# Chunks of at most four gathered rows from a tile pool and a split last superblock, in place of a ring of 50 slots with chunks of up to eight

## The chip, the cores and the metric

The kernel runs on 1 core of one Trainium2 chip. The metric is the device time in microseconds; the time of a kernel is the median of its runs, and lower is better.

## The reference, cut to what matters

A two-layer heterogeneous graph transformer over N = 6250 nodes and E = 100000 edges (sorted by destination), with 16 node types, 32 edge types, width D = 128 and H = 8 heads of 16; around it stands `layernorm(x + gnn(x))`.

```python
def gt_layer(x, ntype, etype, src, dst, Wk, Wq, Wv, Wa, Watt, Wmsg, pri, skip, g, b):
    k = typed_linear(x, ntype, Wk)          # (n, 8, 16); q and v alike
...
    kT = jnp.einsum('nhd,htdo->nhto', k, Watt)      # for each node and edge type
    vT = jnp.einsum('nhd,htdo->nhto', v, Wmsg)
    kw = kT[src, :, etype]
    m = vT[src, :, etype]
    a = jnp.einsum('ehd,ehd->eh', kw, q[dst]) * pri[:, etype].T / SQRT_D
    att = edge_softmax(a, dst, n)
    hag = jax.ops.segment_sum((m * att[:, :, None]).reshape(-1, H * HS), dst, num_segments=n)
    h = jax.nn.silu(typed_linear(hag, ntype, Wa))
    alpha = jax.nn.sigmoid(skip[ntype])[:, None]
    h = h * alpha + x * (1.0 - alpha)
    return normalised(h) * g + b
h = x
for l in range(2): h = gt_layer(h, ...)
return layernorm(x + h @ ff_w + ff_b)
```

## The kernel before, in words

**Prep.** Nodes are ranked by class of types (4 classes of 4 types) and by degree into 50 blocks of 128 nodes, one node to a partition. Block b has `KB[b]` slots, the most incoming edges of any of its nodes: 25, 22, 20, 19, 18, 17, 16, 16, 15, 14 in each class's ten blocks, and 41, 13, 12, 12, 12, 11, 11, 10, 9, 8 in ten blocks of mixed types; 867 in sum. A table in DRAM (`tabs[l]`) holds one row of 256 floats, k and v after `Watt` and `Wmsg`, for every node and edge type. Layer 0's table is written during prep (L1000), in tiles `st` of 2 MB, two to a block.

**Edges of a layer** (`edges(l)`). Blocks come in superblocks of up to four (`sbs`): for each class 4, 3 and 3 blocks, and a superblock of mixed blocks after each of the first three classes, 15 in all. The last two are blocks 34 to 36 and 37 to 39 (K of the latter 16, 15, 14). For each slot of a block one indirect DMA, issued by POOL, gathers 128 rows of the table, one to a partition (L1270): 867 gathers a layer. A block's slots are cut into chunks. For each chunk DVE multiplies k by q (L1282) and sums over each head to `a` (L1286). When all chunks of a block are there, the generator `finished` does the rest: mask, maximum, subtraction, exponential (ACT, L1166), denominators, then the values times weights (L1185), their sum over chunks in `acc` (L1196) and over the chunk's rows (L1201). In layer 0, q, weights and `acc` lie in SBUF; in layer 1 in PSUM (a `tb` tile, `pair`). `finished` of one block is called step by step (`step`) while the next block's chunks are emitted (`before`).

**The ring.** Gathered rows lie in `kvr`, a ring of `SLOTS` = 50 rows. A block's chunks are even, of up to `MOST` = 8 rows, split where the ring ends; 135 chunks a layer. If a slot is still to be read, `finished` of the block before is driven on until its value is added (`used`, `live`).

**Nodes.** After a superblock's last block, the generator `nodes` is put on the list `work`: normalise, transpose, the typed product with `Wa` (L276), silu by tanh, skip, layer norm (`stats`, L1347 and L1350; `rstd_of`), and in layer 0 the next layer's k, v and q (three products, in this order), q written to DRAM (`qrd`). Then `table(pieces_of(...))` puts the pieces of layer 1's table on the list `pieces`: PE products (L297), copies to `st` (ACT, L304; some on DVE, L302), and a scatter by POOL (L1479), `late` by three half steps. `tick` advances `work` and `pieces` at a pace set by the slots of the coming superblocks; `queries` of the next superblock are on `work` too. What is left when the gathers are out is drained at the end of the layer. Layer 1's first gather waits for all scatters of its table. In layer 1, `nodes` ends in `ff_w`, the residual and the last layer norm, giving `o` (L1465); `results` holds its blocks, `leave` counts them down from 7 + 2i and `put_out` writes them by an indirect DMA on POOL (L1512); those of the last superblock are written at once.

**Order.** POOL's instructions run in the order of the program (`manual_schedule` for POOL); an instruction that waits there holds all later gathers, scatters and outs. The other engines' instructions are put in order by the tile framework's scheduler.

Of the kernel before, what the change touches and what calls it, by code (L numbers as in the profile page):

```python
# [9 lines left out]
F32 = mybir.dt.float32  # L10
# [3 lines left out]
ALU = mybir.AluOpType  # L14
# [17 lines left out]
CH = 4  # L32

MOST = 8

SLOTS = 50

# [80 lines left out]
def kernel(  # L118
# [136 lines left out]
    def superblocks(n):  # L255
        k = -(-n // SB)
        for c in range(k):
            yield n * c // k, n * (c + 1) // k - n * c // k
# [773 lines left out]
    def arm(fast):  # L1032
# [4 lines left out]
        STB = 3 if fast else 2  # L1037
        room = [0]
        ep = ctx2.enter_context(tc.tile_pool(name="ep", bufs=2))
        npl = ctx2.enter_context(tc.tile_pool(name="npl", bufs=1))  # L1040
        if fast:
            kvr = npl.tile([P, SLOTS, 2 * D], F32, name="kv")
        eps = npl.tile([P, 1], F32, name="eps")
# [7 lines left out]
        if fast:  # L1051

            mixed = [(NC * CB + i0, k, range(TY)) for i0, k in superblocks(1 + RB)]
            for c in range(NC):
                for i0, k in reversed(list(superblocks(CB))):
                    sbs.append((c * CB + CB - i0 - k, k, range(c * TC, (c + 1) * TC)))
                sbs += mixed[c * len(mixed) // (NC - 1):(c + 1) * len(mixed) // (NC - 1)]
        else:
            sbs = [(i0, k, range(TY)) for i0, k in superblocks(NB)]
# [40 lines left out]
        def edges(l):  # L1100
# [27 lines left out]

            def leave(n):

                for r in results:
                    r[0] -= n
                if results and results[0][0] <= 0:
                    put_out(*results.pop(0)[1])

            def slots(s):
                return sum(KB[b] for b in range(sbs[s][0], sbs[s][0] + sbs[s][1]))

            live = []

# [8 lines left out]

            def finished(s, i, chunks, kvt, used, a, pair, sums, den):  # L1150

# [22 lines left out]
                else:  # L1174
                    acc = pair[:, 0].rearrange("p (k c) -> p k c", k=CH)
                late = []
                for j in range(len(chunks) + 1):
                    more = []
                    if j < len(chunks):
                        j0, j1 = chunks[j]  # L1180
                        v = kvt[j][:, :, D:]
                        parts = [(0, j1 - j0)] if j else [
                            (k0, min(k0 + CH, j1 - j0)) for k0 in range(0, j1 - j0, CH)]
                        for k0, k1 in parts:
                            nc.vector.tensor_tensor(  # L1185
                                (v[:, k0:k1] if j or k0 else acc[:, :k1])
                                .rearrange("p k (h d) -> p k h d", h=H),
                                v[:, k0:k1].rearrange("p k (h d) -> p k h d", h=H),
                                w[:, j0 + k0:j0 + k1, :].unsqueeze(3)
                                .to_broadcast([P, k1 - k0, H, HS]), op=ALU.mult)  # L1190
                        more = [v[:, k0:min(k0 + CH, j1 - j0)]
                                for k0 in range(0 if j else CH, j1 - j0, CH)]
                        yield
                    for v in late:
                        n = v.shape[1]
                        nc.vector.tensor_tensor(acc[:, :n], v, acc[:, :n], op=ALU.add)  # L1196
                    late = more
                    for r in used[:j]:
                        r[2] = True
                    yield  # L1200
# [24 lines left out]
            for s, (i0, k, types) in enumerate(sbs):  # L1225
# [6 lines left out]
                for i in range(k):  # L1232
                    b = i0 + i
                    K = KB[b]
                    a = ep.tile([P, max(KB), H], F32, name="a")
                    if SLOTS - room[0] < CH:
                        room[0] = 0
                    most = min(K, SLOTS - room[0])
                    chunks = []
                    for k0, k1 in ((0, most), (most, K)):  # L1240
                        n = -(-(k1 - k0) // MOST)
                        chunks += [(k0 + (k1 - k0) * j // n, k0 + (k1 - k0) * (j + 1) // n)
                                   for j in range(n)]
                    kvt, used = [], []
                    then = []
# [11 lines left out]
                    for j0, j1 in chunks:  # L1257
                        c = j1 - j0
                        for r in [r for r in live if r[0] < room[0] + c and r[1] > room[0]]:
                            while not r[2]:  # L1260
                                next(before)
                            live.remove(r)
                        live.append([room[0], room[0] + c, False])
                        used.append(live[-1])
                        kv = kvr[:, room[0]:room[0] + c]
                        room[0] = (room[0] + c) % SLOTS
                        kvt.append(kv)
                        for j in range(j0, j1):
# [4 lines left out]
                            if l == 1:  # L1273
# [6 lines left out]
                                puts.clear()  # L1280
                        kk = kv[:, :, :D]
                        nc.vector.tensor_tensor(  # L1282
                            kk, kk, q.unsqueeze(1).to_broadcast([P, c, D]), op=ALU.mult)
                        for r in range(c):
                            if r == c // 3:
                                nc.vector.tensor_reduce(  # L1286
                                    a[:, j0:j1, :], kk.rearrange("p k (h d) -> p k h d", h=H),
                                    axis=AX.X, op=ALU.add)
                            step()
                            tick(1.0)  # L1290
                        leave(c / CH)
                    for _ in before:
                        pass
                    if not then:
                        step(end=True)
                    before = finished(s, i, chunks, kvt, used, a, pair, sums, den)
                    q, pair = then[0] if then else (None, None)
# [55 lines left out]
        def nodes(l, i0, k, types, sums, den, ntb, table):  # L1353
# [45 lines left out]
            if not last:  # L1399
# [22 lines left out]
                elif fast:  # L1422
# [4 lines left out]
                    outs = []  # L1427
                    for j in range(3):
                        ps = nps.tile([P, SB * P], F32, name="nb")
                        outs.append(ps)  # L1430
                        for t, xm in xms:
                            nc.tensor.matmul(ps[:, :n], wkqv[:, j, t, :], xm[:, :n],
                                             start=(t == types[0]), stop=(t == types[-1]))
                        yield
                        if j < 2:
                            to = npl.tile([P, SB * P], F32, name=f"kvT{j}", bufs=2)
                            nc.scalar.copy(to[:, :n], ps[:, :n])
                            outs[j] = to
# [9 lines left out]
                nc.sync.dma_start(rows(qrd[1], i0, k), q[:, :k])  # L1448
                table(pieces_of(i0, k, outs[0], outs[1], (2,) if final else ()))
                return  # L1450
# [229 lines left out]
```

## Time and profile before

| | us |
|---|---|
| median of 3 runs (lowest, highest) | 3686.52 (3684.35, 3697.19) |
| the profiled execution, its own time | 3697.19 |
| the profiled execution, its span | 3695.1 |
| POOL busy, 2213 instructions | 2152.3 |
| DVE busy, 4025 instructions | 1951.6 |
| PE busy | 1808.3 |
| ACT busy | 1018.3 |
| first gather of layer 1 | 2279.99 |

The profiled execution is the highest of the three runs. Busy time leaves out the issue of DMAs and waits. A line of the table of groups has the source line, the engine, the operation, the tiles (out<-in), the count, the busy time, the mean ns of one, and the idle time of the engine ahead of them with what ended it; a line of the waits has engine, tile and line, what ended the wait, us in total, times, longest; a line of a timeline has start, duration, the instruction, and the engine's idle time before it. The granted TensorE clock is 0.64 over the span.

### The profile page before, as it was taken

How to read it: one execution, taken by the hardware profiler on the slowest of the kernel's cores; microseconds unless marked ns; L12 is line 12 of the kernel's file. 1: busy time of each engine (PE TensorE's matmuls, PEld its weight loads, DVE VectorE, ACT ScalarE, POOL GpSimd, SP SyncE). 2: the span in 40 equal slices, each digit the busy share in tenths (PEclk: the TensorE clock that was granted, in tenths of full speed). 3: DMA queues.
4: the chain of work that ended last, by engine and by line, in shares of the span. 5: the costliest groups of instructions: out<-in, count | busy, mean ns of one | idle time of the engine just before them, and what ended most of it. 6: DMA issues, size and time to landing. Idle time of an engine off the chain costs nothing. (4 is left out here: it accounts for less than half of the span.)

```text
span 3695.1 us, 22082 instructions
## 1 busy us (share of the span) xinstructions
PE 1808.3 (49%) x5612; PEld 825.1 (22%) x5612; DVE 1951.6 (53%) x4025; ACT 1018.3 (28%) x1677; POOL 2152.3 (58%) x2213
## 2 busy tenths in 40 slices
PE   3898998115556587668776774012120212113113
PEld 1344545002223233223222221001010101111011
DVE  8665331356356565567456442445554556464545
ACT  2675655002331344123331542001110111111111
POOL 2224654674676666667676543755767557666653
PEclk9788675557667686777768776555555555555555
DMA  6797999634655577456765686332333223333321
GB/s 181 308 387 312 400 403 404 169 99 145 224 188 192 179 266 266 156 171 241 271 220 172 221 307 255 107 87 82 102 93 105 83 86 104 94 90 97 90 82 44
DMA packets 194484, 691.11 MB, mean 187 GB/s; under 512 B 55469, under 2 KB 106032, under 8 KB 169298
## 3 DMA queue, kind: packets, MB, share of 16 engines
q0 software_dynamic: 119120, 651.15, 49.8%
q1 hardware_dynamic: 58838, 31.29, 3.2%
q10 hardware_dynamic: 16384, 7.11, 0.9%
q8 instruction: 48, 0.79, 0.1%
q14 instruction: 94, 0.77, 0.1%
HBM read 264.91 MB, written 429.48 MB: 188 GB/s over the span
## 5 line engine op out<-in xcount | busy, mean ns | idle before, releaser
L1270 POOL DMA_INDIRECT kv<-tab,ell x1734 | 1726.4, 996 | 656.8 <-issue 486.3
L304 ACT COPY st<-tb 128x512 f32<-128x512 f32 (+1 forms) x1064 | 726.4, 758 | 506.7 <-PE tb L297 252.0
L282 PE MATMUL nb<-ident,hag 128*128 128x128 f32 x100 | 25.8, 396 | 765.3 <-DVE hag L1318 207.7
L297 PE MATMUL tb<-bdv,kvT 32*128 32x512 f32 x800 | 283.8, 852 | 96.2 <-ACT st L304 56.9
L297 PE MATMUL tb<-bdv,vT 32*128 32x512 f32 x784 | 296.6, 884 | 28.5 <-ACT st L304 16.9
L1282 DVE TENSOR_TENSOR kv<-kv,q 128x896 f32<-128x896 f32 (+4 forms) x135 | 136.6, 1012 | 315.5 <-DMA kv<-tab,ell 276.2
L276 PE MATMUL nb<-xm,wa 128*128 128x384 f32 (+1 forms) x384 | 236.8, 775 | 131.8 <-DVE xm L267 85.4
L297 PE MATMUL tb<-bdk,kvT 32*128 32x512 f32 x800 | 267.6, 838 | 65.9 <-ACT st L304 46.5
L1479 POOL DMA_INDIRECT tab<-st,row x100 | 105.3, 1053 | 316.4 <-ACT st L304 260.6
L1286 DVE TENSOR_REDUCE a<-kv 128x48 f32<-128x768 f32 (+4 forms) x269 | 270.6, 1007 | 31.3 <-remote 24.2
L267 DVE SCALAR_TENSOR_TENSOR xm<-ntb,nb 128x384 f32<-128x384 bf16 (+1 forms) x336 | 184.7, 595 | 176.5 <-remote 78.0
L297 PE MATMUL tb<-bdk,kT 32*128 32x512 f32 x784 | 257.6, 865 | 0.3 <-ACT st L304 0.3
L1282 DVE TENSOR_TENSOR kv<-kv,tb 128x768 f32<-128x768 f32 (+4 forms) x134 | 136.0, 1015 | 219.4 <-DMA kv<-tab,ell 176.1
L1000 POOL DMA_INDIRECT tab<-st,rows x98 | 103.3, 1054 | 242.4 <-ACT st L304 210.1
L282 PE MATMUL nb<-ident,hs 128*128 128x128 f32 x100 | 37.9, 459 | 328.8 <-DVE hs L1391 158.7
L302 DVE COPY st<-tb 128x512 f32<-128x512 f32 (+1 forms) x120 | 89.1, 745 | 201.6 <-PE tb L297 133.1
L282 PEld LDWEIGHTS nb<-ident,hag 128*128 128x128 f32 x100 | 15.6, 196 | 784.1 <-issue 571.1
L276 PE MATMUL nb<-xm,wq 128*128 128x384 f32 (+1 forms) x192 | 104.6, 707 | 120.3 <-DVE xm L267 108.4
L1512 POOL DMA_INDIRECT out_dram<-o,node x50 | 50.9, 1018 | 192.6 <-DVE o L1465 180.8
L276 PEld LDWEIGHTS nb<-xm,wa 128*128 128x128 f32 x384 | 99.8, 280 | 265.1 <-issue 123.5
L1196 DVE TENSOR_TENSOR tb<-kv,tb 128x512 f32<-128x512 f32 (+3 forms) x211 | 121.9, 578 | 56.2 <-remote 39.2
L1413 PE MATMUL nb<-xm,wkqv 128*128 128x384 f32 (+1 forms) x288 | 122.6, 582 | 39.2 <-DVE xm L267 24.7
(314 smaller groups left out, 2829.8 us busy)
## 6 DMA issues: line engine op xcount, KB each, us to landing
kv<-tab,ell POOLq DMA_INDIRECT x1734
hr<-xrd SPq DMA_DIRECT2D x30, 192.0 KB
hr<-xrd SPq DMA_DIRECT2D x15, 256.0 KB
xrd<-xr POOLq DMA_DIRECT2D x11, 256.0 KB
ntb<-typed SPq DMA_DIRECT2D x20, 96.0 KB
hrd<-hs SPq DMA_DIRECT2D x10, 192.0 KB
qrd<-q SPq DMA_DIRECT2D x10, 192.0 KB
q<-qrd SPq DMA_DIRECT2D x10, 192.0 KB
```

The lines of the kernel that those rows point to most:

```text
L267: nc.vector.scalar_tensor_tensor(xm[:, :n], ntb[:, :n], float(t), hT[:, :n], op0=ALU.is_equal, op1=ALU.mult)
L276: nc.tensor.matmul(ps[:, :n], w[:, t, :], xm[:, :n], start=(t == types[0]), stop=(t == types[-1]))
L297: nc.tensor.matmul(pt[:, b], yT[s, i * P:(i + 1) * P], bd[s, tt, :], start=True, stop=True)
L302: nc.vector.tensor_copy(to, pt)
L304: nc.scalar.copy(to, pt)
L1000: put = nc.gpsimd.indirect_dma_start(out=tabs[0].rearrange("(n t) c -> n (t c)", t=16), out_offset=bass.IndirectOffsetOnAxis(ap=rows1[:, t ...
L1196: nc.vector.tensor_tensor(acc[:, :n], v, acc[:, :n], op=ALU.add)
L1270: get = nc.gpsimd.indirect_dma_start(out=kv[:, j - j0, :], out_offset=None, in_=tabs[l][:], in_offset=bass.IndirectOffsetOnAxis(ap=ell[:, ...
L1282: nc.vector.tensor_tensor(kk, kk, q.unsqueeze(1).to_broadcast([P, c, D]), op=ALU.mult)
L1286: nc.vector.tensor_reduce(a[:, j0:j1, :], kk.rearrange("p k (h d) -> p k h d", h=H), axis=AX.X, op=ALU.add)
L1413: nc.tensor.matmul(outs[j][:, :n], wkqv[:, j, t, :], xm[:, :n], start=(t == types[0]), stop=(t == types[-1]))
L1479: put = nc.gpsimd.indirect_dma_start(out=tabs[1].rearrange("(n t) c -> n (t c)", t=16), out_offset=bass.IndirectOffsetOnAxis(ap=row2[:, tg ...
```

## The change

Chunks are of `CH` = 4 rows with a rest of 1 to 3, as tiles of a pool of 12 buffers of 4 rows (48 rows) in place of the ring, so the framework sets the wait for a free buffer. There are 234 chunks a layer. After each chunk's product and after its sum `step` and `tick` are called, three times a chunk in place of once a row; `finished` yields once a chunk in its value part, with the add of chunk j - 1 behind the product of chunk j, where it yielded twice. `leave` counts by 1 a chunk in place of its rows over 4. The last class's superblocks are of 4, 3, 2 and 1 blocks (16 superblocks in all: the last are blocks 34 to 36, 37 and 38 with K of 16 and 15, and 39 with 14). For the last superblock, `table(pieces_of(...))` stands ahead of the q product.

```diff
...
 BINS = P // NC
 CH = 4
-
-MOST = 8
-
-SLOTS = 50
 def bins_of_degrees(lam):
...
         outs_put, results = [], []
         STB = 3 if fast else 2
-        room = [0]
         ep = ctx2.enter_context(tc.tile_pool(name="ep", bufs=2))
         npl = ctx2.enter_context(tc.tile_pool(name="npl", bufs=1))
-        if fast:
-            kvr = npl.tile([P, SLOTS, 2 * D], F32, name="kv")
         eps = npl.tile([P, 1], F32, name="eps")
         nc.vector.memset(eps, LN_EPS)
...
             mixed = [(NC * CB + i0, k, range(TY)) for i0, k in superblocks(1 + RB)]
             for c in range(NC):
-                for i0, k in reversed(list(superblocks(CB))):
-                    sbs.append((c * CB + CB - i0 - k, k, range(c * TC, (c + 1) * TC)))
+                sizes = [k for _, k in reversed(list(superblocks(CB)))]
+                if c == NC - 1:
+                    sizes = sizes[:-1] + [sizes[-1] - 1, 1]
+                for j, k in enumerate(sizes):
+                    sbs.append((c * CB + sum(sizes[:j]), k, range(c * TC, (c + 1) * TC)))
                 sbs += mixed[c * len(mixed) // (NC - 1):(c + 1) * len(mixed) // (NC - 1)]
         else:
             sbs = [(i0, k, range(TY)) for i0, k in superblocks(NB)]
...
                     for _ in of.pop(0)[0]:
                         pass
-            def leave(n):
+            def leave():
                 for r in results:
-                    r[0] -= n
+                    r[0] -= 1
                 if results and results[0][0] <= 0:
                     put_out(*results.pop(0)[1])
             def slots(s):
                 return sum(KB[b] for b in range(sbs[s][0], sbs[s][0] + sbs[s][1]))
-
-            live = []
             def query(s, i):
...
                 nc.scalar.copy(pair[:, 1, :D], got[s][0][:, i, :])
                 return pair[:, 1, :D], pair
-            def finished(s, i, chunks, kvt, used, a, pair, sums, den):
+            def finished(s, i, chunks, kvt, a, pair, sums, den):
                 i0, k, _ = sbs[s]
...
                     acc = ep.tile([P, CH, D], F32, name="acc", bufs=1)
                 else:
                     acc = pair[:, 0].rearrange("p (k c) -> p k c", k=CH)
-                late = []
                 for j in range(len(chunks) + 1):
-                    more = []
                     if j < len(chunks):
                         j0, j1 = chunks[j]
-                        v = kvt[j][:, :, D:]
-                        parts = [(0, j1 - j0)] if j else [
-                            (k0, min(k0 + CH, j1 - j0)) for k0 in range(0, j1 - j0, CH)]
-                        for k0, k1 in parts:
-                            nc.vector.tensor_tensor(
-                                (v[:, k0:k1] if j or k0 else acc[:, :k1])
-                                .rearrange("p k (h d) -> p k h d", h=H),
-                                v[:, k0:k1].rearrange("p k (h d) -> p k h d", h=H),
-                                w[:, j0 + k0:j0 + k1, :].unsqueeze(3)
-                                .to_broadcast([P, k1 - k0, H, HS]), op=ALU.mult)
-                        more = [v[:, k0:min(k0 + CH, j1 - j0)]
-                                for k0 in range(0 if j else CH, j1 - j0, CH)]
-                        yield
-                    for v in late:
-                        n = v.shape[1]
-                        nc.vector.tensor_tensor(acc[:, :n], v, acc[:, :n], op=ALU.add)
-                    late = more
-                    for r in used[:j]:
-                        r[2] = True
+                        v = kvt[j][:, :j1 - j0, D:]
+                        nc.vector.tensor_tensor(
+                            (v if j else acc).rearrange("p k (h d) -> p k h d", h=H),
+                            v.rearrange("p k (h d) -> p k h d", h=H),
+                            w[:, j0:j1, :].unsqueeze(3).to_broadcast([P, j1 - j0, H, HS]),
+                            op=ALU.mult)
+                    if j > 1:
+                        j0, j1 = chunks[j - 1]
+                        nc.vector.tensor_tensor(acc[:, :j1 - j0], kvt[j - 1][:, :j1 - j0, D:],
+                                                acc[:, :j1 - j0], op=ALU.add)
                     yield
                 nc.vector.tensor_reduce(sums[:, i, :], acc.rearrange("p k c -> p c k"),
                                         axis=AX.X, op=ALU.add)
...
                     b = i0 + i
                     K = KB[b]
                     a = ep.tile([P, max(KB), H], F32, name="a")
-                    if SLOTS - room[0] < CH:
-                        room[0] = 0
-                    most = min(K, SLOTS - room[0])
-                    chunks = []
-                    for k0, k1 in ((0, most), (most, K)):
-                        n = -(-(k1 - k0) // MOST)
-                        chunks += [(k0 + (k1 - k0) * j // n, k0 + (k1 - k0) * (j + 1) // n)
-                                   for j in range(n)]
-                    kvt, used = [], []
+                    chunks = [(j, min(j + CH, K)) for j in range(0, K, CH)]
+                    kvt = []
                     then = []
                     def step(end=False):
...
                     for j0, j1 in chunks:
                         c = j1 - j0
-                        for r in [r for r in live if r[0] < room[0] + c and r[1] > room[0]]:
-                            while not r[2]:
-                                next(before)
-                            live.remove(r)
-                        live.append([room[0], room[0] + c, False])
-                        used.append(live[-1])
-                        kv = kvr[:, room[0]:room[0] + c]
-                        room[0] = (room[0] + c) % SLOTS
+                        kv = ep.tile([P, CH, 2 * D], F32, name="kv", bufs=12)
                         kvt.append(kv)
                         for j in range(j0, j1):
                             at = KO[b] + j
...
                                                              mybir.DependencyReason.DATA),
                                         reason="rows of the table")
                                 puts.clear()
-                        kk = kv[:, :, :D]
+                        kk = kv[:, :c, :D]
                         nc.vector.tensor_tensor(
                             kk, kk, q.unsqueeze(1).to_broadcast([P, c, D]), op=ALU.mult)
-                        for r in range(c):
-                            if r == c // 3:
-                                nc.vector.tensor_reduce(
-                                    a[:, j0:j1, :], kk.rearrange("p k (h d) -> p k h d", h=H),
-                                    axis=AX.X, op=ALU.add)
-                            step()
-                            tick(1.0)
-                        leave(c / CH)
+                        step()
+                        tick(c / 3)
+                        nc.vector.tensor_reduce(a[:, j0:j1, :],
+                                                kk.rearrange("p k (h d) -> p k h d", h=H),
+                                                axis=AX.X, op=ALU.add)
+                        step()
+                        tick(c / 3)
+                        step()
+                        tick(c / 3)
+                        leave()
                     for _ in before:
                         pass
                     if not then:
                         step(end=True)
-                    before = finished(s, i, chunks, kvt, used, a, pair, sums, den)
+                    before = finished(s, i, chunks, kvt, a, pair, sums, den)
                     q, pair = then[0] if then else (None, None)
             for _ in before:
                 pass
...
                     table(None)
                     outs = []
                     for j in range(3):
+                        if final and j == 2:
+                            table(pieces_of(i0, k, outs[0], outs[1], (2,)))
                         ps = nps.tile([P, SB * P], F32, name="nb")
                         outs.append(ps)
                         for t, xm in xms:
...
                 q = yield from q_rows(outs[2], k, "qn")
                 yield
                 nc.sync.dma_start(rows(qrd[1], i0, k), q[:, :k])
-                table(pieces_of(i0, k, outs[0], outs[1], (2,) if final else ()))
+                if not final:
+                    table(pieces_of(i0, k, outs[0], outs[1], ()))
                 return
             h2 = npl.tile([P, SB * P], F32, name="h2", tag="th")
             nc.scalar.copy(h2[:, :n], hT[:, :n])
```

## The prediction

> **What bounds the kernel now.** The table of stages, cut at the layers' first and last gathers (us; busy and count of PE, PEld, DVE, ACT and POOL; clock, DMA share, GB/s), is read first:
>
> ```profile
> 690.00:2194.00 1504.00, 938.08 (x2639) 375.24 (x2641) 845.96 (x1578) 463.04 (x612) 970.39 (x930) 0.69 0.58 202
> 2194.00:2280.00 86.00, 58.57 (x204) 23.10 (x200) 31.80 (x56) 35.91 (x48) 12.58 (x14) 0.72 0.79 319
> 2280.00:3634.00 1354.00, 248.54 (x586) 135.87 (x586) 718.40 (x1504) 137.68 (x275) 867.78 (x910) 0.53 0.32 93
> ```
>
> They are layer 0's edges, the boundary, and layer 1's edges: 2944 of the span's 3695 us. POOL is the busiest engine in both layers, DVE the second. Next the same stretches for the gathers alone, and the groups of instructions and the waits:
>
> ```profile
> 690.00:2194.00 1504.00, 876.83 (x842) 0.69 0.58 202
> 2280.00:3634.00 1354.00, 823.78 (x867) 0.53 0.32 93
> ```
>
> ```profile
> L1270 POOL DMA_INDIRECT kv<-tab,ell x1734 | 1726.4, 996 | 656.8 <-issue 486.3
> ```
>
> ```profile
> DVE kv L1282 <- DMA kv<-tab,ell: 452.3, 95, 22.1
> POOL tab L1479 <- ACT st L304: 260.6, 37, 32.4
> POOL out_dram L1512 <- DVE o L1465: 180.8, 11, 28.3
> ```
>
> A gather is 0.95 us in layer 1 (823.78/867) and 1.04 in layer 0 (876.83/842), and 0.30 us of issue stands ahead of each, 1.25 and 1.34 us a row. Layer 1: 867 x 1.25 = 1084, 43 outs x 1.3 = 56, so POOL waits for 214 us, most of it for o. Layer 0: 842 x 1.34 = 1128, 88 scatters x 1.35 = 119, waits 257, most of it for st. DVE in turn starves 452 us at the head of a chunk. So POOL's rows set the floor, which the change leaves alone (867 rows a layer either way); what it can move are the 471 us of POOL's waits and the boundary.
>
> **Part 1: chunks of at most 4.** The 50 blocks' K give 135 chunks a layer before (6 to 8 rows mostly) and 234 after (200 of 4, 10 of 3, 13 of 2, 11 of 1). L1282 and L1286 go from 270 to 468 each. L1185 goes from 363 to 468 and L1196 from 428 to 368 (chunks less one, in both layers). Together 441 DVE instructions more, over the same elements. What one costs is read from two sizes of one form:
>
> ```profile
> L1282 DVE TENSOR_TENSOR kv<-kv,tb 128x1024 f32<-128x1024 f32 x23 | 28.0, 1219 | 44.0 <-DMA kv<-tab,ell 30.7 <-issue 13.1
> L1282 DVE TENSOR_TENSOR kv<-kv,tb 128x512 f32<-128x512 f32 x6 | 4.1, 684 | 4.2 <-DMA kv<-tab,ell 4.2
> ```
>
> (1219 - 684)/4 = 134 ns a row, so 684 - 4 x 134 = 148, say 0.14 us, is fixed. 441 x 0.14 = **62 us of DVE work**. Where DVE starves it is free; where POOL waits for DVE's results it is in the path. DVE is busy for 53 to 56% of the layers and the waits lie on both sides, so I take half: **+31 (0 to 62)**. The cover is the 452 us of starving; gone, it is 62.
>
> The fixed price is larger in places. The timeline of DVE in layer 1 shows the small instructions of a node chain, in a stretch with gathers running and in one where POOL stands still:
>
> ```profile
> 2451.24 0.29 DVE L1347 BATCH_NORM_STATS2 bn<-hs 128x6 f32<-128x128 f32 x1 [0.41 <-DVE bn L1347]
> 2452.63 0.29 DVE L1347 BATCH_NORM_STATS2 bn<-hs 128x6 f32<-128x128 f32 x1 [1.10 <-DVE bn L1347]
> 2454.03 0.29 DVE L1347 BATCH_NORM_STATS2 bn<-hs 128x6 f32<-128x128 f32 x1 [1.10 <-issue]
> ...
> 2499.50 0.89 DVE L1347 BATCH_NORM_STATS2 bn<-nb 128x6 f32<-128x128 f32 x4 [3.94 <-PE nb L1458]
> ```
>
> Four in 0.89 us while POOL waits at L1512, but one in 1.40 us while it gathers: 1.10 us of gap each, its cause not shown. Marking the stretches in which DVE's instructions keep such gaps gives some 456 of layer 1's 1354 us (39 us in layer 0), and in them the gathers run from 3 to 8 rows ahead of DVE to 20 to 32. A third of layer 1's 220 extra instructions, 74, falls there: 74 x 1.10 = 81 at most; 0 if they only use up slack until the next stall. I take a third, **+27 (0 to 81)**, since the lead absorbs part.
>
> A finer chunk also ends sooner. The product and sum of a block's last chunk take 2 x (0.134 x 6.4 + 0.14) = 2.0 us at the mean 867/135 = 6.4 rows and 1.27 at 3.7, 0.74 less in each of 100 blocks: 74 if every block's end were waited for, 0 if none; a third, **-25 (-74 to 0)**, by the same reasoning. The tile pool's 48 rows against the ring's 50: POOL may lead DVE by 22.0 rows on average where it had 21.3, walking both programs in order (a slot is free once its value add is emitted); **0**. That new wait sits on POOL at L1270, with every later gather, scatter and out behind it.
>
> **Outs.** An out is issued 7 + 2i counts after its o, a count being 4 rows before and one chunk (3.7 rows) after; by walking the order, the first goes 23.0 gathers after its o instead of 24.0. Nine waits for o lie in layer 1, each longer by a pitch: 9 x 1.25 = **+11** (0, if o is early anyway, to 24 for 7 x 0.3 rows). Behind the waiting out stand all gathers. Scatters keep their distance (6.1 gathers for 6.0): 0.
>
> **Part 2: superblocks 4, 3, 2, 1 and pieces ahead of q.** POOL's timeline of the boundary:
>
> ```profile
> 2193.87 0.95 POOL L1270 DMA_INDIRECT kv<-tab,ell  x1 [0.30 <-issue]
> ...
> 2247.20 0.97 POOL L1479 DMA_INDIRECT tab<-st,row  x1 [17.06 <-ACT st L304]
> ...
> 2269.42 0.97 POOL L1479 DMA_INDIRECT tab<-st,row  x1 [3.99 <-ACT tb L1147]
> 2279.99 1.00 POOL L1270 DMA_INDIRECT kv<-tab,ell  x1 [9.60 <-DMA tab<-st,row]
> ```
>
> Twelve tiles of 2 MB follow the last gather, in both versions (6 for blocks 34 to 36, 6 for blocks 37 to 39, walking the order). At 400 to 408 GB/s, the best 100 us windows of the table's DMA, a tile takes 5.2 us and twelve 62, of a gap of 86: 24 to win at most. The 17.06 us wait is for the last superblock's node chain (its k and v are done at 2238); with one block the chain is shorter and its pieces no longer queue behind q's product on PE and its copies on ACT; on POOL no gather of layer 0 is left for the scatters to pass. But the new two-block chain and its q, its qrd write on SP included, now start only after the last gather too: **-16 (-24 to +33**, a whole second chain of 2205.6 to 2238 in series). A sixteenth superblock repeats some 40 small DVE instructions of `nodes` and `queries` in each layer: 80 x 0.14 = 11, half, **+6 (0 to 11)**; its few SP loads have SP idle.
>
> **Tail.** The last gather is at 3633.65, the last out at 3687.94. One block instead of three there shortens the chain's per-block steps: **-5 (-10 to +10)**.
>
> **POOL's gather itself.** It is 0.09 us longer in layer 0, where q, weights and acc lie in SBUF, than in layer 1, where they lie in PSUM. The elements that DVE reads from two SBUF inputs stay the same, so 0. The Trainium skill ("GPSIMD Engine Reference", section 1. Specifications) says that POOL shares its SBUF interfaces with VectorE and contends with DVE instructions of two SBUF inputs. That agrees with 1.04 against 0.95; read per instruction, which speaks against this change, the layer's L1282, L1185 and L1196 rise by 22% (535 to 652) and would add an estimated 0.22 x 842 x 0.09 = 17 us.
>
> **Sum.** 31 + 27 - 25 + 0 + 11 - 16 + 6 - 5 = **+29 us** on the profiled execution, whose own time is 3697.19 (span 3695.1), the highest of the three runs: 3726, or +0.8%. On the median 3686.52 that is **3715 us**.
>
> **The rivals.** (a) The finer grain pays in full: every block's end is waited for, at the block's boundary on DVE, -74 in place of -25. Then 29 - 49 = -20, **3667**, faster. It decides once over half of the 100 block ends reach POOL's waits (0.74 x 65 = 48 takes back the +29 and the 25). For it: POOL's 471 us of waits end on ACT or DVE, whose chains begin at a block's end; against it, 260.6 of them end on st, whose pieces come by count of rows. If also the slow stretches cost nothing it is 3640. (b) The stretches do not grow: 29 - 27 = +2, **3689**, no change. For it: their loss is slack as long as POOL has 20 rows of lead. (c) They pass on all of it: 29 + 54 = +83, **3769**. For it: they end in POOL stalls. (d) The two small chains run in series at the boundary: +33 for -16, **3764**; then the change doesn't do what its second part is for. For it: both are emitted after the last gather; against it, PE and ACT have gaps there (58.57 and 35.91 of 86 us busy).
>
> **How the numbers follow.** The forecast 0.30, (a) 0.27, (b) 0.25, (c) 0.11, (d) 0.07. About 0.5%, 18 us, can be told from no change here. Slower by more: forecast, (c), (d), 0.48; within: (b) less the part that a -16 to -24 boundary takes below, 0.22; faster: (a) and that part, 0.30. The range for 8 in 10 goes from (a) without slow stretches, 3640, to (c) with three quarters of DVE's 62 instead of half, 3769 + 16 = 3785, rounded to 3790. The likeliest case's own range is 3695 to 3740.
>
> **What the profile after would show.** L1282 and L1286 at 468 with means near 0.63 us, DVE's busy time up by 60 us and POOL's gathers at 1.04 and 0.95 still. Right: layer 1 longer by 20 to 50 us, with the excess in POOL's waits for o and for kv, and the boundary near 70. (a): layers' windows shorter. (c): 1.40 us pitches in most of layer 1. (d): a boundary above 100. Wrong altogether if the gathers' own mean moves, or if POOL's waits for st in layer 0 change by more than 50 us, which nothing here prices.

## The result, and the profile after

The changed kernel takes 3703.0 us (median of 20 runs, 3676.47 to 3726.27) against 3683.55 for the kernel before (20 runs beside them): a ratio of 1.0052, with an interval of 1.0029 to 1.0076. It is slower by 19 us. The profiled execution took 3716.7 us, its span is 3714.9.

The stages after, cut at the layers' first and last gathers (columns as in the prediction, the tail added):

```profile
690.00:2207.00 1517.00, 917.86 (x2613) 364.91 (x2613) 860.61 (x1796) 456.12 (x605) 961.20 (x926) 0.70 0.57 197
2207.00:2301.00 94.00, 70.57 (x270) 33.31 (x268) 22.08 (x63) 54.77 (x74) 14.55 (x15) 0.72 0.87 350
2301.00:3648.00 1347.00, 241.13 (x586) 135.03 (x586) 732.56 (x1718) 137.37 (x275) 866.45 (x911) 0.53 0.33 94
3648.00:3715.00 67.00, 22.19 (x64) 14.94 (x64) 32.80 (x110) 18.05 (x28) 6.71 (x7) 0.53 0.05 15
```

Layer 0 is longer (1517 us from 690 where it was 1504), the boundary is longer (94 for 86), layer 1 is shorter (1347 for 1354), the tail longer (67 for 61). DVE has 218 and 214 instructions more in the two layers, yet only 14 to 15 us more of busy time in each. The waits after:

```profile
DVE kv L1251 <- DMA kv<-tab,ell: 310.7, 104, 17.9
POOL tab L1453 <- ACT st L300: 268.4, 43, 17.7
POOL out_dram L1486 <- DVE o L1439: 114.4, 7, 34.1
```

DVE starves 142 us less at the head of a chunk. POOL waits for o 66 us less in the whole run. The gathers themselves, on POOL in layer 0, are no longer (867.93/839 = 1.034 us, where they were 1.041):

```profile
690.00:2207.00 1517.00, 867.93 (x839) 0.70 0.57 197
```

The boundary on POOL, with one scatter more behind the last gather (13 for 12):

```profile
2206.21 1.47 POOL L1239 DMA_INDIRECT kv<-tab,ell  x1 [0.30 <-issue]
...
2222.23 1.98 POOL L1453 DMA_INDIRECT tab<-st,row  x1 [12.28 <-ACT st L300]
...
2258.22 0.97 POOL L1453 DMA_INDIRECT tab<-st,row  x1 [10.98 <-ACT st L300]
...
2287.96 0.97 POOL L1453 DMA_INDIRECT tab<-st,row  x1 [12.30 <-ACT q L1077]
2290.47 0.97 POOL L1453 DMA_INDIRECT tab<-st,row  x1 [1.54 <-ACT tb L1141]
2300.84 0.99 POOL L1239 DMA_INDIRECT kv<-tab,ell  x1 [9.40 <-DMA tab<-st,row]
```

Before, a second long wait stood ahead of the 17.06 us that the prediction shows:

```profile
2217.61 0.98 POOL L1479 DMA_INDIRECT tab<-st,row  x1 [13.41 <-ACT st L304]
```

So two long waits (13.41 and 17.06 us) have become three (12.28, 10.98 and 12.30), the last two ahead of the first scatter of each of the two last superblocks. All waits ahead of the boundary's scatters come to 70 us where they were 64. The rows of the stages show a second difference: 94 us at 350 GB/s are 33 MB, where 86 us at 319 GB/s were 27 MB, so more of the table is left for the boundary. Why the last wait comes is seen in the timelines of DVE and PE. The last block's `hag` is there at 2225.63, and PE transposes it only at 2263.20, behind the two-block superblock's k, v, q product and its pieces:

```profile
2225.63 0.29 DVE L1289 TENSOR_TENSOR hag<-sums,rd 128x128 f32<-128x128 f32 x1
```

```profile
2244.84 6.80 PE L1405 MATMUL nb<-xm,wkqv 128*128 128x256 f32 x24
...
2263.20 0.47 PE L278 MATMUL nb<-ident,hag 128*128 128x128 f32 x1
```

### The profile page after: what moved, and what is told of

The parts are those of the page before. It is cut to its first block, busy times and chain, and to the rows that moved or that the text cites. A ratio compares the mean times of both kernels' runs of the same rounds, so it can differ in the third digit from the quotient of the medians.

```text
span 3714.9 us, 22671 instructions
## 1 busy us (share of the span) xinstructions
PE 1791.2 (48%) x5660; PEld 821.3 (22%) x5660; DVE 1979.9 (53%) x4496; ACT 1036.3 (28%) x1706; POOL 2144.5 (58%) x2213
## 5 line engine op out<-in xcount | busy, mean ns | idle before, releaser
L263 DVE SCALAR_TENSOR_TENSOR xm<-ntb,nb 128x384 f32<-128x384 bf16 (+3 forms) x352 | 188.1, 573 | 321.2 <-remote 179.1
L272 PE MATMUL nb<-xm,wa 128*128 128x384 f32 (+3 forms) x400 | 246.3, 773 | 221.1 <-DVE xm L263 127.7
L1255 DVE TENSOR_REDUCE a<-kv 128x32 f32<-128x512 f32 (+3 forms) x468 | 298.7, 641 | 47.0 <-remote 16.9
L293 PE MATMUL tb<-bdv,kvT 32*128 32x512 f32 x800 | 273.0, 814 | 69.0 <-ACT st L300 35.1
L293 PE MATMUL tb<-bdv,vT 32*128 32x512 f32 x784 | 283.9, 860 | 28.1 <-ACT st L300 14.0
L293 PE MATMUL tb<-bdk,kvT 32*128 32x512 f32 x800 | 255.7, 820 | 75.8 <-ACT st L300 49.9
L1251 DVE TENSOR_TENSOR kv<-kv,q 128x512 f32<-128x512 f32 (+3 forms) x234 | 151.0, 648 | 227.7 <-DMA kv<-tab,ell 194.2
L1251 DVE TENSOR_TENSOR kv<-kv,tb 128x512 f32<-128x512 f32 (+3 forms) x234 | 149.9, 644 | 125.1 <-DMA kv<-tab,ell 116.5
L272 PE MATMUL nb<-xm,wq 128*128 128x384 f32 (+3 forms) x200 | 100.0, 653 | 148.4 <-issue 86.3
L1141 ACT COPY tb<-q 128x128 f32<-128x128 f32 x50 | 13.4, 269 | 520.1 <-DVE a L1255 136.6
```

Of the source, the lines that this page charges most:

```text
L263: nc.vector.scalar_tensor_tensor(xm[:, :n], ntb[:, :n], float(t), hT[:, :n], op0=ALU.is_equal, op1=ALU.mult)
L272: nc.tensor.matmul(ps[:, :n], w[:, t, :], xm[:, :n], start=(t == types[0]), stop=(t == types[-1]))
L293: nc.tensor.matmul(pt[:, b], yT[s, i * P:(i + 1) * P], bd[s, tt, :], start=True, stop=True)
L1251: nc.vector.tensor_tensor(kk, kk, q.unsqueeze(1).to_broadcast([P, c, D]), op=ALU.mult)
L1255: nc.vector.tensor_reduce(a[:, j0:j1, :], kk.rearrange("p k (h d) -> p k h d", h=H), axis=AX.X, op=ALU.add)
```

## The experiments

The experiments ran in three groups, each on one chip with its own runs of the kernel before, and comparisons are within a group: before took 3676.8 us in the first, 3349.5 in the second and 3675.82 in the third. The second chip is another case, and this turned out to matter most; each chip was used in one group alone, so what is the chip's and what the occasion's isn't told apart. Stages by the starts of the first and last gathers of each layer, in one profile each; "stretches" is the time in which the signals of DVE's completions come in steps of 0.70 us (the gaps that the prediction showed). Where a stretch begins and ends is not sharp, and the figures for layer 1 are good to some tens of us:

| kernel | group | layer 0 | boundary | layer 1 | tail | stretches, layer 0 / 1 |
|---|---|---|---|---|---|---|
| before | (first measured) | 1535.9 | 86.1 | 1353.7 | 61.4 | 39 / 456 |
| after | (first measured) | 1551.6 | 94.6 | 1347.0 | 67.1 | 118 / 555 |
| chunks_alone | 1 | 1549.2 | 87.0 | 1344.4 | 74.3 | 130 / 563 |
| blocks_and_pieces | 1 | 1537.0 | 97.3 | 1353.3 | 62.1 | 39 / 475 |
| pieces_alone | 1 | 1515.8 | 84.1 | 1349.1 | 61.2 | 23 / 510 |
| blocks_442 | 1 | 1521.8 | 81.3 | 1344.7 | 61.3 | 31 / 479 |
| ring_4_l0 | 2 | 1347.2 | 88.5 | 1152.3 | 58.6 | 0 / 0 |
| ring_4_l1 | 2 | 1386.0 | 86.7 | 1148.3 | 50.0 | 0 / 0 |
| sum_twice | 2 | 1394.6 | 87.2 | 1162.1 | 56.8 | 0 / 0 |
| outs_later | 2 | 1386.6 | 82.0 | 1147.9 | 60.9 | 0 / 0 |
| after_again | 3 | 1538.3 | 91.5 | 1343.5 | 76.1 | 96 / 548 |
| chunks_again | 3 | 1532.9 | 92.4 | 1344.5 | 72.5 | 92 / 625 |
| ring_4 | 3 | 1561.8 | 92.3 | 1355.3 | 66.3 | 139 / 577 |
| ring_4_442 | 3 | 1552.8 | 87.8 | 1353.8 | 62.2 | 146 / 590 |

Layer 0 varies by some 20 us between executions of nearly the same code (1515.8 to 1537.0 in the four with chunks of up to 8 that are not of group 2); for the same code, the boundary varies by some 5 us (87.0 and 92.4 for part 1 alone, 94.6 and 91.5 for the whole), the tail by up to 9, layer 1 by some 3.

**chunks_alone: part 1 alone.** The changed kernel with `sbs` and the place of `table(pieces_of(...))` put back.

```diff
-                sizes = [k for _, k in reversed(list(superblocks(CB)))]
...
+                for i0, k in reversed(list(superblocks(CB))):
+                    sbs.append((c * CB + CB - i0 - k, k, range(c * TC, (c + 1) * TC)))
...
-                        if final and j == 2:
-                            table(pieces_of(i0, k, outs[0], outs[1], (2,)))
```

> Part 1 alone: chunks of at most 4 from the tile pool, the last class still in superblocks of 4, 3, 3 and its pieces behind q. By the prediction's sum (31 + 27 - 25 + 11 = +44 us of chunks and outs) the time is 1.2% above before, and the boundary keeps its 86 us. By the rival read from the two profiles (the excess of the change sits in the boundary, +8.5, and the tail, +5.7 us; layer 0 +15.7 and layer 1 -6.7 us, so +9 us for the chunks) it is within 0.5% of before, below the whole change.

Measured: 1.0046 (1.0018 to 1.0073), 3692.68 us. Part 1 costs 16 us, not 44. The boundary keeps its length (87.0) here; in the second profile of this kernel, in the third group, it is 92.4.

**blocks_and_pieces: part 2 alone**, the kernel before with the two edits that the last run undid.

> Part 2 alone: the ring of 50 and chunks of up to 8 stay, the last class is in superblocks of 4, 3, 2, 1, and the last one's pieces stand ahead of q. By the prediction (-16 at the boundary, -5 at the tail, half of +6) some 18 us or 0.5% below before, boundary near 70 us. By the rival (the node chains of the last two superblocks run one after the other): boundary 90 to 100 us, tail 65 to 68 us from last gather to end in place of 61, and 10 to 15 us or 0.3 to 0.4% above before.

Measured: 1.0040 (1.0017 to 1.0064), 3690.03 us. Part 2 by itself is slower, and its boundary is the longest of all (97.3). The boundary is as long as the rival of two chains in series had it; the tail isn't (62.1). In this run, too, the last `hag` is early (2202.13) and the last chain's product late (2257.76), behind the other superblock's:

```profile
2205.63 7.56 PE L1437 MATMUL nb<-xm,wkqv 128*128 128x256 f32 x24
2227.78 0.33 PE L282 MATMUL nb<-ident,hag 128*128 128x128 f32 x1
2257.05 0.33 PE L282 MATMUL nb<-ident,hs 128*128 128x128 f32 x1
2257.76 4.54 PE L1437 MATMUL nb<-xm,wkqv 128*128 128x128 f32 x24 [0.38 <-DVE xm L267]
```

There is another candidate beside the second chain: 14 scatters lie behind the last gather here, 13 in the changed kernel, and 12 in every kernel of the table whose last class is not in superblocks of 4, 3, 2 and 1. At the prediction's 5.2 us a tile, the further tiles are an estimated 10 us of the 11 by which this boundary is longer. The two weren't tried apart.

**pieces_alone: only the pieces ahead of q**, superblocks 4, 3, 3.

> Only the last superblock's pieces ahead of its q, superblocks 4, 3, 3 and ring as before. Its q product, copy, transposition and copy took from 2237.8 to 2242.4 between the end of v and the first copies to st, so the first scatter behind the chain comes 3 to 5 us sooner, and the boundary is 81 to 83 us in place of 86 by the rival of serial chains, which blames the split alone; by a theory that the order of pieces and q is what costs, the boundary is 90 us or longer. The time changes by 0.1%, which this can't tell.

Measured: 0.9984 (0.9954 to 1.0014), no difference that can be told; boundary 84.1. So the order of pieces and q does no harm, and the loss of part 2 is the split, by whichever of the two ways.

**blocks_442: a short last superblock without a chain ahead of it**, pieces ahead of q.

```diff
+                if c == NC - 1:
+                    sizes = [4, 4, 2]
```

> The last class in superblocks of 4, 4, 2 (no sixteenth superblock), pieces ahead of q, ring and chunks as before. If what costs in the change is a second node chain behind the last gather, a short last superblock without that chain should gain: 4 tiles instead of 6 behind the chain (2 x 5.2 = 10 us) and 3 to 5 us of q: boundary 70 to 75 us, the time 0.3 to 0.5% below before. By the prediction's theory of the split (its gain is the smaller last superblock, whatever stands ahead) it gains 16 us as well and doesn't differ from part 2 alone.

Measured: 0.9970 (0.9949 to 0.9991), 3665.33 us, faster. The boundary is 81.3, not 70 to 75: eight scatters now stand ahead of the last chain's wait, where six did. That is 5 us of the 11; where the rest lies isn't shown, since layer 0 varies by more. Its last scatters:

```profile
2228.25 0.97 POOL L1485 DMA_INDIRECT tab<-st,row  x1 [8.92 <-ACT q L1084]
2230.85 0.97 POOL L1485 DMA_INDIRECT tab<-st,row  x1 [1.62 <-DVE st L302]
2234.76 0.98 POOL L1485 DMA_INDIRECT tab<-st,row  x1 [2.94 <-DVE st L302]
2240.01 0.97 POOL L1485 DMA_INDIRECT tab<-st,row  x1 [4.28 <-ACT tb L1150]
2251.46 0.99 POOL L1273 DMA_INDIRECT kv<-tab,ell  x1 [10.47 <-DMA tab<-st,row]
```

The wait for the chain is 8.92 us for 17.06. A shorter last superblock halves this wait; with another short one in front of it, waits of 11 and 12 us stand in its place.

**ring_4_l0: chunks of 4 in layer 0 alone**, in the ring, on the second chip.

```diff
+                        if l == 0:
+                            chunks += [(j, min(j + CH, k1)) for j in range(k0, k1, CH)]
+                            continue
```

> The kernel before with chunks of at most 4 in layer 0 alone; the ring, the step for each row and the superblocks stay. With part 1 alone, layer 0 was 13 us longer than before in the one profile of each, layer 1 and the tail together 4 us. If the cost of part 1 is the smaller chunk's DVE work in layer 0: 0.3 to 0.5% above before (11 to 18 us), DVE's busy time in layer 0 up by 30 us. By the prediction's terms for one layer (half of 31, less half of 25) it is +3 us, no change. If the cost lies in the tile pool and its steps and not in the size, no change either, and the next run tells no more.

Measured: 0.9874 (0.9854 to 0.9893), faster by 1.3%; none of the theories had it. **ring_4_l1** is the same edit for layer 1.

> The kernel before with chunks of at most 4 in layer 1 alone. By the prediction (15 of DVE's fixed cost, 27 in the slow stretches, less 12 for the finer grain) +30 us, 0.8% above before. By the theory that POOL's waits in layer 1 only change their name (for o 132 before, 59 with part 1; for a free buffer 77 and 139) and that the stretches are slack: within 0.2% of before, layer 1 with its tail within 10 us of 1415, and the stretches of slow DVE instructions over 550 us in place of 495 of the whole run.

Measured: 0.9952 (0.9934 to 0.9969), faster by 0.5%. On this chip the kernel before is 327 us shorter than in the first group, and no stretch of slow DVE instructions is found in any of the four profiles. In layer 1, with gathers running, DVE's small instructions stand close (ring_4_l1):

```profile
2351.26 0.69 DVE L1285 TENSOR_TENSOR kv<-kv,tb 128x512 f32<-128x512 f32 x1 [4.39 <-DMA kv<-tab,ell]
2351.86 0.69 DVE L1185 TENSOR_TENSOR tb<-kv,tb 128x512 f32<-128x512 f32 x1
2352.46 0.69 DVE L1350 BATCH_NORM_STATS2 bn<-nb 128x6 f32<-128x128 f32 x3
```

In the changed kernel as first measured, idle gaps of 1.4 to 1.5 us stand ahead of two in three of them, in the same kind of code:

```profile
2412.67 0.70 DVE L1181 TENSOR_TENSOR tb<-kv,tb 128x512 f32<-128x512 f32 x1 [1.42 <-issue]
2413.27 0.68 DVE L1251 TENSOR_TENSOR kv<-kv,tb 128x512 f32<-128x512 f32 x1
2415.47 0.69 DVE L1174 TENSOR_TENSOR kv<-kv,tb 128x512 f32<-128x512 f32 x1 [1.52 <-issue]
```

The stages of ring_4_l0 and then of ring_4_l1, layer 0 in each (chunks of 4, then of up to 8):

```profile
690.00:1996.00 1306.00, 886.33 (x2597) 358.15 (x2598) 853.31 (x1789) 454.74 (x604) 950.00 (x924) 0.73 0.66 232
```

```profile
690.00:2034.00 1344.00, 889.28 (x2625) 363.38 (x2627) 838.83 (x1567) 458.53 (x609) 963.56 (x922) 0.72 0.65 226
```

With 222 DVE instructions more and 14 us more of DVE work, the layer is 38 us shorter. The gathers account for part of it: 1.024 us each (855.91/836) against 1.046 (872.52/834), 18 us of the 38. Why they are shorter isn't shown. POOL's waits for st in the layer, each counted above the 0.30 us of issue that stands ahead of any, are 65 us for 86, another 21.

**sum_twice: more DVE work**, each chunk's sum a second time into a tile that nobody reads.

```diff
+                                again = ep.tile([P, MOST, H], F32, name="again", bufs=1)
+                                nc.vector.tensor_reduce(
+                                    again[:, :c], kk.rearrange("p k (h d) -> p k h d", h=H),
+                                    axis=AX.X, op=ALU.add)
```

> The kernel before with each chunk's sum over heads done a second time into a tile that nobody reads: 270 DVE instructions and 271 us of DVE work more, half in each layer. It measures how much of added DVE work comes through. By the prediction's half: +135 us, 3822 on a median of 3687, in both layers alike. By the theory that layer 1 has slack and layer 0 has not: layer 0 longer by 90 us or more, layer 1 by under 40. If DVE's starving (452 us) hides it: under 30 us in all.

Measured: 1.0031 (1.0016 to 1.0045), 10 us for 270 us of instructions, so 4% comes through and not half. DVE's starving hides it. This holds on the second chip; on a chip with stretches it wasn't tried.

**outs_later: the outs 7 counts later**, on top of blocks_442.

```diff
-                    results.append([7 + 2 * i, (o, i0, i)])
+                    results.append([14 + 2 * i, (o, i0, i)])
```

> Superblocks 4, 4, 2 and pieces ahead of q as in the run before, and the outs of a superblock counted from 14 + 2i in place of 7 + 2i, so that POOL reaches an out some 28 rows later. The waits for o in layer 1 (109 us in 8) should fall below 30. If those waits are what holds layer 1, it is shorter by 50 us or more, and the time 1.5% below before. If a wait for o only takes the place of a wait for a free slot of the ring, as part 1 alone suggests, the waits at the gathers rise from 92 to 160 us or more, and layer 1 stays within 15 us of 1345.

Measured: 0.9955 (0.9938 to 0.9972) against the kernel before. It doesn't answer its question: on the second chip POOL doesn't wait for o inside layer 1 at the old distance either (ring_4_l1 keeps 7 + 2i, and both of its waits for o, 34 us, lie in the tail). What it shows is that superblocks of 4, 4, 2 with the pieces ahead are faster there too, with this distance; layer 1 is 1147.9.

**after_again**: the changed kernel, third group.

> The changed kernel once more. Where it was first measured, the kernel before takes 3677 to 3687 us and DVE's instructions stand 0.7 or 1.4 us apart in some 500 us of it; in the runs with chunks of 4 in one layer, the kernel before took 3349.5 us and no such stretch was found. If the sign of the change hangs on these stretches: on a chip with them 0.5% above before again; on a chip without them below before, by about 1.3% + 0.5% for the two layers less 0.4% for part 2, so 1 to 1.7% below. If the pool and its steps cost what the ring does not, it is above before on either.

Measured: 1.0083 (1.0049 to 1.0118); this chip has the stretches. Slower, as at first; in this group by 11 us more than part 1 alone (3706.51 and 3695.33).

**chunks_again**: part 1 alone, third group.

> Part 1 alone once more (tile pool, 4-3-3 superblocks). On a chip with the stretches 0.5% above before; on one without them, if the size of the chunk is what matters, 1.3 to 1.8% below before like the ring with chunks of 4; if the tile pool and its three steps a chunk cost something, less than that by the cost.

Measured: 1.0053 (1.0031 to 1.0075), as in the first group. The boundary is 92.4 us without the split and was 91.5 with it in after_again: beside chunks of 4, a longer boundary by the split isn't seen in this group, and where the 11 us between the two kernels lie isn't shown.

**ring_4: chunks of at most 4 in the ring, both layers.**

> The kernel before with chunks of at most 4 in both layers, ring and a step for each row. On a chip without the stretches the two layers add up: 1.3% + 0.5% = 1.7% below before. On a chip with them: 0.5% above before if the smaller chunk is the cost of part 1, no change or below if the pool is.

Measured: 1.0140 (1.0106 to 1.0174), 3733.39 us. The edit that is faster in either layer on the second chip is 1.4% slower here. And it is slower than chunks_again, 3695.33 on the same chip: with chunks of at most 4 in both, the rest of part 1 (the tile pool, three steps a chunk in place of one a row, the new `finished` and `leave`) is worth 38 us; which of these isn't shown. The stages of ring_4:

```profile
690.00:2220.00 1530.00, 941.19 (x2604) 371.68 (x2604) 861.85 (x1801) 456.79 (x603) 959.42 (x930) 0.69 0.57 198
2220.00:2312.00 92.00, 68.90 (x237) 27.04 (x237) 31.69 (x59) 42.97 (x56) 12.60 (x14) 0.72 0.76 307
2312.00:3667.00 1355.00, 249.43 (x586) 135.53 (x586) 731.65 (x1722) 136.50 (x275) 865.04 (x910) 0.53 0.32 93
```

Layer 0 of ring_4_l0 has 1306 us with nearly the same DVE work (853 us) and POOL work (950); here it takes 1530. What differs is waiting: POOL waits for st 230 us in place of 65 and at the gathers 57 in place of 10, counted as above. PE is busy for 941 us in place of 886 as well, at a clock of 0.69 for 0.73.

**ring_4_442**: the same with superblocks 4, 4, 2 and pieces ahead.

> Chunks of at most 4 in the ring with superblocks 4, 4, 2 and pieces ahead of q: the best of what was seen on either chip. Without stretches 2.0% below before (1.7% and 0.3%); with them between 0.3% below and 0.2% above. Boundary 80 to 83 us, as with 4, 4, 2 alone (81.3).

Measured: 1.0066 (1.0044 to 1.0088): above the range that was expected, since ring_4 was dearer than thought; below ring_4 by 32 us, so the superblocks of 4, 4, 2 with the pieces ahead pay here as well.

## Why the prediction was right, and where it wasn't

Slower by 0.8% was forecast and 0.5% came (0.8% in the third group), but the sum came out by errors that cancel, which is luck: part 1 was priced at +44 and cost 16 to 20; part 2 at -15 (boundary, tail, chain) and cost 13 by itself. The parts don't add up either: 29 us together, where the whole cost 19 at first and 31 in the third group. Of the signs that the prediction named, the 468 instructions a group, their means (0.64 us) and the gathers' means came. Layer 1 longer by 20 to 50 us, DVE's busy time up by 60 us and a boundary near 70 us did not.

**The count of instructions** was right: DVE has 4496 where it had 4025, 441 and the extra chain's. **Their fixed price** was too high. 0.14 us was read from durations, and neighbours on DVE overlap: two instructions of 0.69 us start 0.60 apart (2351.26 and 2351.86 above). DVE's busy time rose by 28.3 us (1979.9 for 1951.6), 28.3/471 = 0.06 us for each, not by 62; in part 1 alone it rose by 36 us for 443, 0.08 each. The durations themselves were as read (683 ns at 4 rows):

```profile
L1251 DVE TENSOR_TENSOR kv<-kv,tb 128x512 f32<-128x512 f32 x200 | 136.4, 683 | 122.9 <-DMA kv<-tab,ell 114.3 <-issue 8.5
```

The share that comes through, half, failed as well where it could be measured alone: 4% in sum_twice.

**The slow stretches** were named, but their place was wrong: the term stood for layer 1. There they grew from 456 us before (up to 510 in the other profiles with chunks of up to 8) to between 548 and 625, and layer 1 with its tail did not (1415.1 before; 1414.1 and 1419.6 after; 1418.7 and 1417.0 for part 1), so no cost of them is seen there; that is rival (b)'s price, though (b) had them not grow. In layer 0, where the prediction put nothing, they grew from 39 to between 92 and 130 us, and layer 0 is longer in three of four profiles of part 1 or the whole than in any of the four with chunks of up to 8. That the stretches are the cause fits the two kinds of chip and is argued, not shown: on the second chip the clock (0.66 for 0.64), PE's busy time and POOL's waits differ too. What makes them was not found, and so what part 1's 16 to 20 us come of stays open.

**The finer grain**, -25 with -74 as its end, was never measured by itself. On the second chip, with all costs in it, chunks of 4 gain 1.3% in layer 0 and 0.5% in layer 1, 44 and 17 us, more than even rival (a) had in net; but 18 us of it are shorter gathers, and that the rest comes of blocks that end sooner isn't shown. The changed kernel itself was not run on that chip. Rival (a)'s own sum was off as well: taking back the +29 and the 25, 54 us at 0.74 each, needs 73 of the 100 block ends and not 65.

**The wait moved to the gather** was put at 0 and the outs at +11. In layer 1, POOL's waits for o (counted above the 0.30 us of issue) fell from 132.2 to 60.0 us and its waits at the gathers rose from 77.3 to 143.5: the wait for a free buffer takes the place of the wait for o, -6 in sum. Walking the order gives nearly the same mean lead for both (21.3 and 22.0 rows), and so didn't see this.

**The boundary** is the step that failed in part 2: -16 was forecast, +8.5 came (+5 in the second profile of the changed kernel, +11 in part 2 alone). Rival (d) had the direction: the split makes two node chains that both start behind the last gather, and the second stands behind the first one's pieces on PE and ACT. But its sign, a boundary above 100 us, did not come, and the twelve tiles that the prediction took for both versions are 13 and 14 with the split. How much is the chain's and how much the tiles' stays open. The tail was forecast 5 shorter and is 6 longer (15 in the second profile); part 2 alone leaves it (62.1) and part 1 alone lengthens it (74.3), so it comes with part 1: more of DVE's work is left behind the last gather (46 us of instructions by their durations in that tail, 30 before), while layer 1 is 9 us shorter.

**The gather's own time** stayed, as forecast. The Trainium skill ("GPSIMD Engine Reference", section 1. Specifications) has POOL contend with VectorE's instructions of two SBUF inputs. Read per instruction, that was an estimated 17 us more in layer 0, and 1.041 became 1.034 us. Over the whole layer the mean is 1.020 to 1.038 us in the profiles with chunks of 4 there and 1.036 to 1.060 in those with chunks of up to 8: the number of such instructions is not what sets it.

## What to carry to other kernels

Read an instruction's price from the starts of neighbours, not from its duration, and let added work on an engine that starves come through by what a run shows. When the last part of a pipeline is split, look for what the new chain stands behind and how much work is left to it: here a shorter last piece gained where no new piece came beside it (4, 4, 2 is faster than 4, 3, 3) and lost where one did (4, 3, 2, 1). A wait removed at one instruction of an in-order queue may come back at the next, so add up all of the queue's waits.

## What was not expected of the hardware

The same kernel took 3677 us on two chips and 3349.5 on a third, where POOL waits 86 us for st in layer 0 in place of 226 (ring_4_l1, whose layer 0 is as before), hardly for o or a free slot in layer 1 (18 us even in sum_twice, in place of 210), and where DVE's completions never come in steps of 0.70 us. Where the stretches are, the trace also has fewer completion signals than instructions that send one (before: DVE 2867 for 3791, PE 2113 for 2566, ACT 1234 for 1571); on the third chip none of DVE's is missing (3783 for 3783 in outs_later). So what ended a wait is told less surely where the stretches are, and whether the two have one cause isn't known. The sign of one edit differs with the chip: chunks of 4 in the ring cost 1.4% together on the one kind, and gain 1.3% and 0.5% in the two layers on the other. Of what was tried, superblocks of 4, 4, 2 with the pieces ahead of q, with chunks as before, are faster than the kernel before on either kind: 0.9970 (0.9949 to 0.9991) of its time in the first group, and with later outs 0.9955 (0.9938 to 0.9972) in the second.
